# Layers 1 and 2 of the likelihood as 32x32 products in differing array tiles, with attention that subtracts its maxima

## The chip, the cores and the metric

The kernel runs on one NeuronCore of one Trainium2 chip. The metric is the device time of one execution in microseconds. A core has five engines that run side by side, each with its own queue in fixed order: TensorE (PE; PEld is its loading of weights), VectorE (DVE), ScalarE (ACT), GpSimd (POOL) and SyncE (SP), which issues most DMAs. PE writes to PSUM, a small memory of eight banks; DVE and ACT read it from there.

## What is computed

Two layers over x of shape 4 x 192 x 128 x 128 (batch, channels, 16384 pixels as tokens). The first is an attention block over tokens that are sorted by cluster; the second gives each value a likelihood.

```python
# layer 0, per image: tokens xn = layernorm(x^T), sorted by the nearest of 64 means
out1 = attn(q, k window of 256 keys, v window)      # groups of 128 queries, 8 heads of 24
out2 = attn(q, kg, vg)                              # 64 global keys per head
out = unsort(out1 + out2) @ Wproj @ Wconv
xt = x + out
h1 = layernorm(xt) @ W_fc1                          # 384 channels
xt = xt + gelu(depthwise_conv3x3(h1)) @ W_fc2
# layer 1, per channel: a chain of small maps, for lower = x - 0.5 and upper = x + 0.5
for i, (M, b) in enumerate(zip(Ms, bs)):            # 3x1, 3x3, 3x3, 1x3
    x = einsum('coi,cin->con', softplus(M), x) + b
    if i < 3:
        x = x + tanh(fs[i]) * tanh(x)
s = -sign(lower + upper)
result = maximum(abs(sigmoid(s * upper) - sigmoid(s * lower)), 1e-9)
```

`attn` is a softmax attention with scale 24 ** -0.5. In the likelihood a channel has three hidden values, so the maps of layers 1 and 2 are 3x3 per channel: 192 channels give 576 rows, and each map is block-diagonal.

## The kernel before

Everything is 32-bit. The program is written with a scheduling library that fixes the order of each engine's queue when it is built; buffers come from pools, and an instruction that takes a buffer waits for its last reader. PSUM has two rings: `ps1` gives one-bank tiles, four in number, and `ps2` gives two-bank tiles, two in number.

First weights are prepared. Then, for each of the four images, come these stages (functions by name):

- `cluster` normalises the tokens, finds each one's mean and its rank (lines 442 to 526); `order` scatters token numbers with 128 indirect DMAs on POOL (L533). Image 0's and 1's clustering comes at the start, that of images 2 and 3 before attention of images 1 and 2; `order` of the next image is issued beside `attention` of this one.
- `attention` (L628) walks 32 blocks of 512 sorted tokens. `fetch` gathers them (POOL, L553), `project` makes queries, keys and values (L562 to L564, L658 to L660), and for each tile of 128 keys `weigh` forms the scores `st` (eight products of 26 rows in different row tiles, L680) and `se` against the global keys (L689), and takes Exp on ACT (L683, L692). `gather` multiplies with the values (L705, L708), `divide` transposes (L719) and divides by the sums. Each step of the loop, `advance(g)`, does `weigh(g)`, `divide` of an older tile and `gather(g - 2)`. There are 4 x 128 tiles.
- `finish` (L758) walks 32 blocks of 512 pixels: `expand(i)`, `convolve(i - 1)`, `likelihood(i - 2)`. `expand` gathers the attention result, adds the residual, normalises and does fc1 (L787 to L800). `convolve` is nine multiply-adds per channel group on DVE (L821). `likelihood` does fc2 (L836) and the four maps.

The maxima. Softmax is taken without subtracting a maximum where a bound says that this is safe. The preparation computes such a bound from Gram matrices of the weights (`grams`, L182) and leaves a 0 or 1 in `wide`; the function `shifts` (L566), which computes maxima and writes them to `shifts_d` in memory, stands in a branch on it (L927). `project` loads the shifts from there into two spare rows per head of the queries (L645 to L649); they are zero when the branch isn't taken. In the profiled execution no instruction of `shifts` is in the trace.

The likelihood. Forty channels make a group of 120 rows; there are five groups, the last of 96 rows. Layer 0 is one product per group into a `ps1` tile (L859). Layers 1 and 2 are two products per group, one per side (lower, upper), with a 120x120 block-diagonal matrix (L866):

```python
ps = ps2(f"h{layer}_{n}_{g}")
for s in range(2):
    mm(ps[:m, s, :], lhsT=lw[:m, g].rearrange("p c o -> p (c o)")[:, :m],
       rhs=us[g][:m, s, :], start=True, stop=True)
us[g] = bend(g, layer, ps)
```

`bend` takes tanh of each side on ACT (L850) and then one multiply-add of both sides on DVE (L852), from PSUM; only then is the `ps2` tile free for the next group but one. Layer 3 (L874) sums three and two groups, and L878 to L888 make the likelihood with ACT, POOL and DVE.

A 32-bit product is two records in the trace, [...]so that L866 with 2 layers x 128 blocks x 10 products has 5120.

Of the kernel before, what the change touches and what calls it, by code (L numbers as in the profile page):

```python
# [31 lines left out]
R = 3 * G  # L32
NG = 5
HR = 32
LN_EPS = 1e-5
BOUND = 1e-9
SAFE = 60.0
# [3 lines left out]
def conv_seq_kernel(  # L41
# [73 lines left out]
    l0a = const([CA, 3, G, 3], "l0a")  # L115
    l0b = const([CB, 2, G, 3], "l0b")
    l1w = const([R, NG, G, 3], "l1w")
    l2w = const([R, NG, G, 3], "l2w")
    l3a = const([R, 3, CA], "l3a")
    l3b = const([R, 2, CB], "l3b")  # L120
    gate = const([R, 3, NG], "gate")
    bias = const([R, 3, NG, 2], "bias")
# [3 lines left out]
    def rows_of(g):  # L126
        return R if g < NG - 1 else 3 * (C - (NG - 1) * G)

    shifts_d = [dram.tile([8, 2, N], F32, tag=f"sh_d{b}", name=f"sh_d{b}") for b in range(B)]
    wide = const([1, 1], "wide", I32)

    with tc.tile_pool(name="prep", bufs=2) as prep:
# [42 lines left out]

        bounds = prep.tile([P, 2, 2], F32, bufs=1)  # L180

        def grams(parts, name):  # L182

            out = prep.tile([P, 2, HR], F32, tag=name, name=name, bufs=1)
            for t in range(2):
                ps = ps1("ps_gram")
                for k, part in enumerate(parts):
                    w = part[:, t].rearrange("p h e -> p (h e)")
                    mm(ps[:, 0:P], lhsT=w, rhs=w, start=k == 0, stop=k == len(parts) - 1)
                for h in range(4):  # L190
                    r = slice(HR * h, HR * h + HR)
                    nc.vector.tensor_copy(out[r, t], ps[r, r])
            return out

        gram_q = grams((q0, q1), "gram_q")
        gram_k = grams((k0, k1), "gram_k")
        nc.vector.tensor_tensor(gram_k, gram_k, gram_q, ALU.mult)
        nc.vector.tensor_reduce(bounds[:, 0], gram_k, AX.X, ALU.add)
# [54 lines left out]
        kgt = prep.tile([M, 2, 4, HR], F32, bufs=1)  # L253
        for t in range(2):
            ps = ps1("ps_kgt")
            mm(ps[:M, 0:P], lhsT=ma[:, 0, :], rhs=kp0[:, t].rearrange("p h e -> p (h e)"), start=True, stop=False)
            mm(ps[:M, 0:P], lhsT=mb[:, 0, :], rhs=kp1[:, t].rearrange("p h e -> p (h e)"), start=False, stop=True)
            nc.vector.tensor_copy(kgt[:, t].rearrange("p h e -> p (h e)"), ps[:M, 0:P])
        gram_m = grams((kgt,), "gram_m")
        nc.vector.tensor_tensor(gram_m, gram_m, gram_q, ALU.mult)  # L260
        nc.vector.tensor_reduce(bounds[:, 1], gram_m, AX.X, ALU.add)

        both = prep.tile([P, 2], F32, bufs=1)
        nc.vector.tensor_scalar_mul(both, bounds[:, 1], float(C + 1))
        nc.vector.scalar_tensor_tensor(both, bounds[:, 0], float(C + 1) ** 2, both, ALU.mult, ALU.add)
        ps = ps1("ps_bound")
        mm(ps[:, 0:2], lhsT=ones, rhs=both, start=True, stop=True)
        total = prep.tile([1, 1], F32, bufs=1)
        nc.vector.tensor_reduce(total, ps[0:1, 0:2], AX.X, ALU.add)
        nc.vector.tensor_scalar(total, total, SAFE * SAFE, None, ALU.is_le)  # L270
        nc.vector.tensor_scalar(total, total, -1.0, 1.0, ALU.mult, ALU.add)
        nc.vector.tensor_copy(wide, total)
        zeros = prep.tile([P, 16 * N // P], F32, bufs=1)
        nc.vector.memset(zeros, 0.0)
        for sh_d in shifts_d:
            nc.sync.dma_start(out=sh_d.rearrange("k t (a n) -> (k t a) n", n=16 * N // P), in_=zeros)
# [30 lines left out]

        NS = 8 * NG + 6
        raw = prep.tile([P, NS], F32, bufs=1)
        nc.vector.memset(raw, 0.0)  # L310
        rawg = raw[:, 0:8 * NG].rearrange("p (g e) -> p g e", e=8)
        vecs = prep.tile([R, 6, NG], F32, bufs=1)
        nc.vector.memset(vecs, 0.0)
        m0r = m0.rearrange("c (o u) -> (c o) u", u=1)
        for g in range(NG):
            n = rows_of(g)
            s = slice(g * R, g * R + n)
            nc.sync.dma_start(out=rawg[:n, g, 0:1], in_=m0r[s, :])
            nc.sync.dma_start(out=rawg[:n, g, 1:4], in_=m1[s, :])
            nc.sync.dma_start(out=rawg[:n, g, 4:7], in_=m2[s, :])  # L320
            nc.sync.dma_start(out=rawg[:n, g, 7:8], in_=m3[s, :])
            for e, v in enumerate((b0, b1, b2, f0, f1, f2)):
                nc.sync.dma_start(out=vecs[:n, e, g:g + 1], in_=v[s, :])
        nc.sync.dma_start(out=raw[:CA, 8 * NG:8 * NG + 3], in_=m0[0:CA, :])
        nc.sync.dma_start(out=raw[:CB, 8 * NG + 3:NS], in_=m0[CA:C, :])
        sp = prep.tile([P, NS], F32, bufs=1)
        e1 = prep.tile([P, NS], F32, bufs=1)
        u1 = prep.tile([P, NS], F32, bufs=1)
        c1 = prep.tile([P, NS], F32, bufs=1)
        nc.scalar.activation(e1, raw, AF.Abs)  # L330
# [297 lines left out]
    def attention(b, xn_d, idx, beside):  # L628

        at_d = dram.tile([N, C], F32, tag="at_d", bufs=2, name=f"at_d{b}")  # L630
        with tc.tile_pool(name=f"at{b}", bufs=2, reuse_waits="tile") as pool:
# [104 lines left out]
            def advance(g):  # L736
                if g < NT:
                    weigh(g)
# [237 lines left out]
```

## Time and profile before

| what | value |
|---|---|
| time, median of 3 runs | 14425.05 us (14421.28 to 14430.82) |
| profiled execution: time | 14425.05 us |
| profiled execution: span | 14423.3 us |
| mean granted PE clock | 0.885 of full |
| PE busy | 11673.1 us (81%) |
| DVE busy | 7433.7 us (52%) |
| ACT busy | 6510.6 us (45%) |
| POOL busy | 3611.5 us (25%) |
| L852, gates on DVE | 2416.4 us, 1920 of 1274 ns |
| L850, tanh on ACT | 2397.7 us, 3840 of 684 ns |
| L866, layers 1 and 2 on PE | 1204.4 and 1193.0 us, 2560 records each |
| L821, convolution on DVE | 2500.4 us, 5304 of 518 ns |

A share of the whole span is a mean over stages with different limits. So the stages have to be looked at one by one, and in each the question is which engine's queue has no gaps. Durations of one operation include its latency; two that follow each other on an engine start closer together than that. `idle before <- X` names what ended an engine's wait.

### The profile page before, as it was taken

The page shows a single profiled execution, that of the slowest core. Times are in us where ns is not written, and L with a number is a line of the kernel's source. Part 1 is how long each engine was busy: PE and PEld are TensorE (multiplying, and loading weights), DVE is VectorE, ACT ScalarE, POOL GpSimd, SP SyncE. Part 2 cuts the span into 40 slices and gives each one's busy share as a digit, 9 for nine tenths or more (in the row PEclk, how much of TensorE's full clock was granted, in tenths as well). Part 3 has the DMA queues.
Part 4 walks back from the last instruction along what each step waited for, and adds up shares of the span by engine and source line. Part 5 has one row for each costly group of instructions (what it writes and reads, how often), then busy time and mean ns, then how long its engine had stood idle before and what let it go on. Part 6 is the DMA issues. An engine that isn't in the chain of part 4 may idle for free. (4 is left out here: it accounts for less than half of the span.)

```text
span 14423.3 us, 161829 instructions
## 1 busy us (share of the span) xinstructions
PE 11673.1 (81%) x60928; PEld 5960.0 (41%) x60928; DVE 7433.7 (52%) x14065; ACT 6510.6 (45%) x9595; POOL 3611.5 (25%) x3991
## 2 busy tenths in 40 slices
PE   7658888888877888888887788888888888788888
PEld 5535543333354554333335455433333455333333
DVE  5611137777762113777775211477777111577776
ACT  1124445555522444555552244455555444455555
POOL 1443222222213322222212432222221222222222
PEclk6579999999967999999996799999999999899999
DMA  2200000000021000000002000000000000000000
GB/s 84 73 15 24 26 27 19 18 20 19 14 62 28 24 25 27 19 19 18 19 13 66 24 26 24 27 20 18 19 19 12 23 26 25 26 19 18 20 19 10
DMA packets 302035, 373.88 MB, mean 26 GB/s; under 512 B 58590, under 2 KB 208542, under 8 KB 300702
## 3 DMA queue, kind: packets, MB, share of 16 engines
q1 hardware_dynamic: 235678, 262.11, 6.1%
q0 software_dynamic: 65536, 101.02, 2.7%
q8 instruction: 491, 8.04, 0.2%
q14 instruction: 330, 2.70, 0.1%
HBM read 207.51 MB, written 155.45 MB: 25 GB/s over the span
## 5 line engine op out<-in xcount | busy, mean ns | idle before, releaser
L850 ACT ACTIVATE t_f<-h_f,bias 120x512 f32<-120x512 f32 (+1 forms) x3840 | 2397.7, 684 | 1711.6 <-PE h_f L866 1311.5
L821 DVE SCALAR_TENSOR_TENSOR acc_f<-hd_f,dwt,acc_f 128x128 f32<-128x128 f32 (+2 forms) x5304 | 2500.4, 518 | 568.1 <-ACT hd_f L800 521.3
L852 DVE SCALAR_TENSOR_TENSOR u_f<-t_f,gate,h_f 120x1024 f32<-120x1024 f32 (+1 forms) x1920 | 2416.4, 1274 | 244.0 <-ACT t_f L850 241.2
L866 PE MATMUL h_f<-u_f,l2w 120*120 120x512 f32 (+1 forms) x2560 | 1204.4, 606 | 247.5 <-DVE u_f L852 247.4
L683 ACT ACTIVATE es<-st 128x1024 f32<-128x1024 f32 (+1 forms) x1024 | 990.3, 1018 | 657.2 <-PE st L680 630.1
L722 DVE RECIPROCAL rec<-ao 128x16 f32<-128x16 f32 x512 | 131.9, 258 | 2143.4 <-PE ao L719 2102.5
L866 PE MATMUL h_f<-u_f,l1w 120*120 120x512 f32 (+1 forms) x2560 | 1193.0, 605 | 28.8 <-DVE u_f L852 28.8
L768 POOL DMA_INDIRECT at_f<-at_d,pos x512 | 615.1, 1201 | 2150.8 <-PE pb_gf L435 1900.7
L660 DVE COPY va_a<-pv_a 128x512 f32<-128x512 f32 x256 | 176.9, 692 | 1622.7 <-PE pv_a L659 1572.5
L728 POOL TENSOR_TENSOR ot<-on 128x192 f32<-128x192 f32 x512 | 303.5, 593 | 2544.4 <-DVE on L724 2541.1
L880 POOL TENSOR_TENSOR sg_f<-lu_f 120x512 f32<-120x512 f32 (+1 forms) x256 | 383.4, 1498 | 2186.5 <-ACT lu_f L878 2176.8
L798 PE MATMUL ph_f<-ta_f,fc 128*128 128x512 f32 x768 | 608.6, 886 | 395.7 <-ACT ta_f L433 395.7
L882 DVE TENSOR_TENSOR lu_f<-lu_f,sg_f 120x1024 f32<-120x1024 f32 (+1 forms) x256 | 317.4, 1240 | 1081.0 <-ACT sg_f L881 1081.0
L689 PE MATMUL se<-qt_a,kgx 64*128 64x128 f32 x4096 | 379.4, 305 | 596.0 <-ACT es L683 590.1
L866 PEld LDWEIGHTS h_f<-u_f,l2w 120*120 120x120 f32 (+1 forms) x2560 | 417.4, 178 | 1011.7 <-DVE u_f L852 627.0
L712 ACT COPY sums<-av 128x512 f32<-128x512 f32 x512 | 300.1, 586 | 1122.3 <-PE av L708 1031.1
L874 PE MATMUL h_f<-u_f,l3a 120*120 120x512 f32 x1536 | 692.2, 600 | 128.4 <-DVE u_f L852 128.4
L866 PEld LDWEIGHTS h_f<-u_f,l1w 120*120 120x120 f32 (+1 forms) x2560 | 441.3, 180 | 746.7 <-issue 602.6
L705 PE MATMUL av<-es,va_a 128*32 128x128 f32 x16384 | 712.9, 287 | 1.3 <-issue 1.3
L680 PE MATMUL st<-qt_a,kt_a 26*128 26x256 f32 (+1 forms) x8192 | 702.8, 406 | 3.0 <-issue 2.6
L836 PE MATMUL py_f<-acc_f,fc 128*120 128x512 f32 (+1 forms) x1536 | 680.7, 592 | 0.0
L533 POOL DMA_INDIRECT idx_d<-tok,pos x512 | 501.4, 979 | 700.9 <-DMA idx_d<-tok,pos 610.2
(307 smaller groups left out, 19364.0 us busy)
## 6 DMA issues: line engine op xcount, KB each, us to landing
xn_d<-xn_c SPq DMA_DIRECT2D x128, 384.0 KB
at_d<-ot SPq DMA_DIRECT2D x128, 384.0 KB
xa_c<-in_x SPq DMA_DIRECT2D x128, 256.0 KB
xa_f<-in_x SPq DMA_DIRECT2D x128, 240.0 KB
out<-pm_f SPq DMA_DIRECT2D x128, 240.0 KB
xb_f<-in_x SPq DMA_DIRECT2D x128, 144.0 KB
out<-pm_f SPq DMA_DIRECT2D x128, 144.0 KB
xb_c<-in_x SPq DMA_DIRECT2D x128, 128.0 KB
```

What stands on the lines that cost most here:

```text
L533: nc.gpsimd.indirect_dma_start(out=idx_d[:, :], out_offset=bass.IndirectOffsetOnAxis(ap=pos[:, t:t + 1], axis=0), in_=tok[:, t:t + 1], in_ ...
L680: mm(psv[:, h, t, :], lhsT=kt[r, t, ks], rhs=qt[r, t, c0 + q0_:c0 + 2 * P], start=True, stop=True)
L683: nc.scalar.activation(e[:, :, :, q0_:], psv, AF.Exp)
L705: mm(av[HR * r:HR * r + HR, 0, t, :], lhsT=blocks[k // NJ][2][:, k % NJ, 4 * t + r, :], rhs=es[r // 2][:, r % 2, t, c0:c0 + P], start=w == ...
L768: nc.gpsimd.indirect_dma_start(out=at[:, j, :], out_offset=None, in_=at_d[:, :], in_offset=bass.IndirectOffsetOnAxis(ap=pos[:, t:t + 1], a ...
L798: mm(ps, lhsT=fc1_0[:, s], rhs=ta, start=True, stop=False)
L821: nc.vector.scalar_tensor_tensor(acc[:, k, r0:r1, :], src[:, k, s0:s0 + r1 - r0, dx:dx + W], dwt[:, k, t:t + 1], acc[:, k, r0:r1, :], ALU. ...
L836: mm(ps[:m], lhsT=fc2[:, k, s], rhs=acc[:, k].rearrange("p r w -> p (r w)"), start=k == 0, stop=k == 2)
L850: nc.scalar.activation(t[:m, s, :], src[:m, s, :], AF.Tanh, bias=bias[:m, layer, g, s:s + 1])
L852: nc.vector.scalar_tensor_tensor(u[:m], t[:m], gate[:m, layer, g:g + 1], src[:m], ALU.mult, ALU.add)
L866: mm(ps[:m, s, :], lhsT=lw[:m, g].rearrange("p c o -> p (c o)")[:, :m], rhs=us[g][:m, s, :], start=True, stop=True)
L874: mm(ps[:m, s, :], lhsT=part[:r, k], rhs=us[g][:r, s, :], start=k == 0, stop=k == len(gs) - 1)
```

## The change

Two things differ from the kernel before.

In the likelihood, layers 1 and 2 become products of 32x32: a set of ten channels (30 of 32 rows) and one side each. A group of 40 channels lies as four sets in the four quarters of the 128 partitions, so a group and layer takes eight products. `turn` moves the output of layer 1 by a number of quarters that depends on group and side, so that the eight products of a group, and those of two groups in a row, fall into different 32x32 tiles of the array; layer 2 moves them back. Since the two sides then lie in different quarters, bias and gate get a side too, and the gate of layer 1 is two instructions of 512 elements. All tiles have 128 rows.

```diff
-                    t = pool.tile([R, 2, NB], F32, tag="t", bufs=2, name=f"t_{n}_{g}_{layer}")
+                    t = pool.tile([P, 2, NB], F32, tag="t", bufs=2, name=f"t_{n}_{g}_{layer}")
                     for s in range(2):
-                        nc.scalar.activation(t[:m, s, :], src[:m, s, :], AF.Tanh, bias=bias[:m, layer, g, s:s + 1])
-                    u = pool.tile([R, 2, NB], F32, tag="u", bufs=6, name=f"u_{n}_{g}_{layer}")
-                    nc.vector.scalar_tensor_tensor(u[:m], t[:m], gate[:m, layer, g:g + 1], src[:m], ALU.mult, ALU.add)
+                        nc.scalar.activation(t[:, s, :], src[:, s, :], AF.Tanh, bias=bias[:, layer, g, s:s + 1])
+                    u = pool.tile([P, 2, NB], F32, tag="u", bufs=6, name=f"u_{n}_{g}_{layer}")
+
+                    for v in ([slice(0, 1), slice(1, 2)] if layer == 1 else [slice(0, 2)]):
+                        nc.vector.scalar_tensor_tensor(u[:, v], t[:, v], gate[:, layer, g, v.start:v.start + 1],
+                                                       src[:, v], ALU.mult, ALU.add)
...
-                        for s in range(2):
-                            mm(ps[:m, s, :], lhsT=lw[:m, g].rearrange("p c o -> p (c o)")[:, :m],
-                               rhs=us[g][:m, s, :], start=True, stop=True)
+                        for q in range(Q):
+                            for s in range(2):
+                                r = 32 * ((q + turn(layer - 1, g, s)) % Q)
+                                c = 32 * ((q + turn(layer, g, s)) % Q)
+                                w = l1w[r:r + 32, g] if layer == 1 else l2w[r:r + 32, g, s]
+                                mm(ps[c:c + 32, s, :], lhsT=w, rhs=us[g][r:r + 32, s, :], start=True, stop=True)
                         us[g] = bend(g, layer, ps)
```

```python
def turn(layer, g, s):
    return 2 * (g % 2) + s if layer == 1 else 0
```

In attention the bound, the branch, `shifts` and `shifts_d` are gone; the maxima are computed in every case, inside the loop. `maxima(g)` forms the scores of 128 queries against 256 keys and against the global keys and reduces them on DVE; `shift(g)` transposes the maxima and subtracts them from the queries, once for each of the two key tiles that meet them (`pair`). `weigh` runs one tile later.

```diff
             def advance(g):
-                if g < NT:
-                    weigh(g)
+                mx = maxima(g) if g < NT else None
+                if 1 <= g <= NT:
+                    weigh(g - 1)
                 if late:
                     divide(*late.pop())
-                if 2 <= g < NT + 2:
-                    late.append((g - 2, gather(g - 2)))
+                if 3 <= g < NT + 3:
+                    late.append((g - 3, gather(g - 3)))
+                if mx is not None:
+                    shift(g, mx)
```

```python
def maxima(g):
    ...
    mx = pool.tile([P, 2, 4, HR], F32, tag="mx", name=f"mx{b}_{g}")
    nc.gpsimd.memset(mx, 0.0)
    for a in range(2):
        ps = ps2(f"sm{b}_{g}_{a}")
        psv = ps.rearrange("p h (t e) -> p h t e", t=2)
        for t in range(2):
            for h in range(2):
                r = slice(HR * (2 * a + h), HR * (2 * a + h) + D)
                mm(psv[:, h, t, 0:n], lhsT=qt[r, t, qs], rhs=kt[r, t, c0:c0 + n], start=True, stop=True)
        nc.vector.tensor_reduce(
            mx[:, :, 2 * a:2 * a + 2, D].rearrange("p t h -> p h t"), psv[:, :, :, 0:n], AX.X, ALU.max)
    ps = ps1(f"sg{b}_{g}")
    for t in range(2):
        mm(ps[:, t * 256:(t + 1) * 256], lhsT=qt[:, t, qs],
           rhs=kgx[:, t].rearrange("p h m -> p (h m)"), start=True, stop=True)
    nc.vector.tensor_reduce(mx[:, :, :, D + 1], ps.rearrange("p (t h m) -> p t h m", t=2, m=M),
                            AX.X, ALU.max)
    return mx

def shift(g, mx):
    ...
    for t in range(2):
        nc.tensor.transpose(pmv[:, t, :], mx[:, t].rearrange("p h e -> p (h e)"), ident)
    nc.vector.tensor_tensor(pair(g)[:, :, 1, :], qt[:, :, qs], pmv, ALU.subtract)
    if g + 1 < NT:
        nc.vector.tensor_tensor(pair(g + 1)[:, :, 0, :], qt[:, :, qs], pmv, ALU.subtract)
```

The buffers of the exponentials `es` go from eight to six, those of `eg` from four to three. In the preparation the small weights are loaded with fewer, longer DMAs, built per set of ten channels on partitions 0 to 31 and copied to their quarters.

## The prediction

> **What bounds the kernel now.** I read the page's slices first, then the groups, then each engine's timeline over one steady stretch of each stage.
>
> ```profile
> PE   7658888888877888888887788888888888788888
> DVE  5611137777762113777775211477777111577776
> PEclk6579999999967999999996799999999999899999
> ```
>
> Four pairs of stages are seen. Where DVE is at 1 it is attention (about 1130 us each: its L680 runs from 889 to 2014, 4464 to 5594, 8048 to 9175 and 11277 to 12342). Where DVE is at 7 it is the finish stage (about 2030 us each), which ends in the likelihood. Clustering fills the rest.
>
> ```profile
> 1400.00:1900.00 500.00, 434.35 (x4641) 274.67 (x4642) 68.30 (x148) 229.80 (x327) 104.74 (x148) 1.00 0.09 25
> 2200.00:3900.00 1700.00, 1396.96 (x3357) 550.98 (x3358) 1228.02 (x2055) 916.23 (x1359) 404.55 (x368) 0.91 0.07 18
> ```
>
> The columns are length, then PE, PEld, DVE, ACT and POOL busy, then clock. Attention is PE's alone: 87% against 14% on DVE. Finish has PE at 82% and DVE at 72%, and which of them is the bound is not read from such means. One query tile of attention, from the timeline of PE:
>
> ```profile
> 1505.71 1.16 PE L680 MATMUL st<-qt_a,kt_a 26*128 26x256 f32 x16
> 1507.97 0.72 PE L689 MATMUL se<-qt_a,kgx 64*128 64x128 f32 x8 [1.10 <-ACT es L683]
> 1508.62 0.66 PE L719 MATMUL ao<-ident,sums 128*128 128x128 f32 x4
> ...
> 1511.13 1.16 PE L680 MATMUL st<-qt_a,kt_a 26*128 26x256 f32 x16
> ```
>
> The loop takes 5.42 us per tile, with one wait of 1.1 us for Exp to free a two-bank PSUM buffer; projections add some 3.6 us per tile (1130 us / 128 tiles = 8.8). In finish a block of 512 pixels repeats every 63.5 us. Its DVE, while layers 1 and 2 run:
>
> ```profile
> 2957.18 1.66 DVE L821 SCALAR_TENSOR_TENSOR acc_f<-hd_f,dwt,acc_f 128x384 f32<-128x384 f32 x3
> 2959.13 1.28 DVE L852 SCALAR_TENSOR_TENSOR u_f<-t_f,gate,h_f 96x1024 f32<-96x1024 f32 x1 [0.29 <-ACT t_f L850]
> 2960.32 0.61 DVE L821 SCALAR_TENSOR_TENSOR acc_f<-hd_f,dwt,acc_f 128x384 f32<-128x384 f32 x1
> 2960.85 1.28 DVE L852 SCALAR_TENSOR_TENSOR u_f<-t_f,gate,h_f 120x1024 f32<-120x1024 f32 x1
> ...
> 2970.36 1.28 DVE L852 SCALAR_TENSOR_TENSOR u_f<-t_f,gate,h_f 96x1024 f32<-96x1024 f32 x1 [0.31 <-ACT t_f L850]
> 2978.86 1.23 DVE L882 TENSOR_TENSOR lu_f<-lu_f,sg_f 120x1024 f32<-120x1024 f32 x1 [7.22 <-ACT sg_f L881]
> ```
>
> From 2930.4 to 2971.6 DVE has only four gaps, 0.21, 0.44, 0.29 and 0.31 us: 1.25 us of 41. The convolution's L821 stands in its queue between the gates L852. PE, in the same stretch, waits for it:
>
> ```profile
> 2965.22 3.81 PE L866 MATMUL h_f<-u_f,l2w 120*120 120x512 f32 x8 [1.06 <-DVE u_f L852]
> 2970.10 5.41 PE L874 MATMUL h_f<-u_f,l3a 120*120 120x512 f32 x12 [1.07 <-DVE u_f L852]
> ```
>
> So DVE, not PE, sets the pace of layers 0 to 2. Only from L874 on (some 22 us of the block) does PE's time and the chain behind it count, and none of that is made shorter.
>
> **What the Trainium skill says.** "TensorEngine Tiling (Array Packing)", Key Properties: different array tiles load weights and multiply in parallel. The trace agrees: L680's records of 256 columns in four row tiles cost 702.8 us / 8192 = 86 ns each, against 406 ns for one from start to end and about 213 ns of streaming (half of L836's 430 ns pitch at 512 columns). The same page, PSUM Bottleneck: tiling speeds up TensorE but not the evacuation of PSUM. That is this finish stage. "TensorE: Matmul & The Clock Gate", Part 1: the clock falls to half after a window of 3413 ns that counts as idle. The trace agrees on the window and shows that half idle is enough:
>
> ```profile
> 2598.80:2602.21 3.41, 1.03 (x6) 1.00 0.00 0
> 2602.21:2605.62 3.41, 0.81 (x4) 0.50 0.16 32
> 2609.04:2612.45 3.41, 3.41 (x5) 0.50 0.00 0
> ```
>
> Here 30% busy (first figure after the length) was followed by half clock, which ended only after a full window. The window before these, 55% busy, kept the clock; one of 53% (1230.09 to 1233.51) lost it.
>
> **The change, part by part.**
>
> *Layers 1 and 2.* Removed: 20 products per block, 40 records, at 430 ns: (1204.4 + 1193.0) / 128 = 18.7 us of PE. Added: 80 products, 160 records, with eight different tiles per group. A tile runs two records of 427 ns, eight tiles side by side: about 0.9 us per group instead of 1.87, so 9 us per block; 4.7 if two groups fill all sixteen. PE gives up 9 to 14 us. On the path this is worth only what DVE waited, 1.25 us at most; walking the after order through DVE's queue (one L821 now stands between the last two gates) I find L874 starting 0.9 us earlier. The split of layer 1's gate into two halves costs nothing: starts of 512-element operations are 0.60 us apart (L789), of 1024-element ones 1.19. Rows 120 to 128 cost no time. Sum: -0.9 us x 128 = -115 us.
>
> *What a faster PE triggers.* A group arrives every 2.2 to 2.5 us and PE is busy about 1.0 of it (with its latency): 40 to 45%, below the half that kept the clock. I expect half clock by the end of layer 2. There it hides (1.8 us per group is what DVE's pace allows today), but L874 begins at half clock and has to wait for one aligned full window: 3.4 to 6.8 us at half speed, 1.7 to 3.4 us lost, all on the path to L878, L880, L882. With four chances in five: +2.0 us; some 0.3 us more where L787/L788 are caught. +2.3 x 128 = +295 us. If the clock holds, this is 0. Finish together: +180 us.
>
> *Attention with maxima.* Added per query tile on PE: eight products like L680 (0.96 us for sixteen records), two like L658 with 256 columns (4 x 0.21 = 0.85), two transposes (0.3, L719). On DVE: two reductions of 1024 (L523: 1.21 each), one of 512 (about 0.69, between L480 and L523), two subtractions of 256 (0.42, L482). DVE has room, but the two-bank PSUM buffers are two, and now take five users in a row instead of three: the score products wait for both reductions. Walked through: scores of the maxima 0 to 1.15; subtractions for the tile before end at 1.06; first reduction 1.25 to 2.5, second to 3.65; first `st` 2.6 to 3.45, its Exp to 4.77, second `st` 3.75 to 4.6; `se` 4.85 to 5.5; `ao` to 6.1, `av` to 8.0 (1.92 today), transposes to 8.3. With the reductions starting 0.2 us earlier it is 8.05. Instead of 5.42: +2.65 to +2.9, I take +2.75 x 512 = +1410 us. Bounds: +2.1 (PE work alone, the stall overlapped) and +3.6 (each wait once more): +1075 to +1850.
>
> *Gone or moved.* 1024 small loads of shifts on SP, the copy on POOL (its like for keys stays), the memset of `mx` on POOL (no such row; bounded by 0.3 to 0.6 us, ahead of the reductions by a tile). In three attentions POOL also issues `idx_d` at 2.4 us each, 128 times; they lost some 65 us each by it (1130 against 1064 in the fourth). A longer tile covers part: -60 us over three. The branch before each attention goes; clustering's tail (DVE alone for 27 us, PE idle) may overlap the next gather in two stages: -40, bounded by 0 and -60. Preparation: 50 loads become 20 at 0.43 us, the wait for the branch value goes: -15. Together -115.
>
> Sum: +1410 + 180 - 115 = +1475, on 14423.3 us of span and 1.75 us around it, which is the median of the runs as well: 15,900 us.
>
> **The rivals.**
> 1. The clock holds, or is regained in time: finish gains 115 to 190. 15,570 to 15,600. For it: four-row work in attention keeps 1.00. Against: a DVE-paced PE is below half busy.
> 2. Attention stalls once more per tile (the ring of two buffers, POOL's memset behind an `idx_d`): +3.6 us per tile and half clock there at times, 16,350. For it: POOL is at 50% in the first third; against: the memset is two tiles ahead.
> 3. The other side: PE's saving comes off finish in full, because groups no longer wait and DVE's gaps close. With sixteen tiles at once 14 us x 128 = 1790: 14,425 + 1410 - 115 - 1790 = 13,930. It decides from 10.2 us per block. For it: PE at 82% and DVE at 72%. Against: DVE's 41 us without gaps; L866 could vanish and that queue would still take 40.
> 4. Half of that: 4.5 us per block, as by a shorter tail: 15,150.
>
> **How the numbers follow.** 0.58 for the forecast, 0.22 for rival 1, 0.11 for 2, 0.04 for 3, 0.05 for 4. The forecast's own spread (2.4 to 3.1 us per tile, finish 0 to +400) is 15,600 to 16,200; with rival 1 and some of 2 the range is 15,500 to 16,250. A measurement of this kernel tells 0.2% (29 us) from nothing; only rival 3 is faster: 0.04, none ends within 0.2% (0.01), slower 0.95.
>
> **What would show it.** Right: attention near 1480 us each, DVE there near 45%, a wait of the score products for DVE's reductions; L866's successor at 9 us per block or less, DVE's stretch of 41 us nearly unchanged, a finish stage within 5% of 2030 us, PEclk lower there, and L874's records slower. Wrong: a finish below 1900 us (then PE was the bound), a clock of 0.91 or more there, or a tile loop outside 7.5 to 9 us.

## The result, and the profile after

The changed kernel takes 16190.95 us (median of 4 runs, 16156.76 to 16230.05), the kernel before 14423.17 us (14418.51 to 14430.82, 4 runs). The ratio is 1.1226, with a 95% interval of 1.1199 to 1.1253: slower by 12.3%, 1768 us. The profiled execution took 16156.76 us (span 16154.7), 1731 us more than that of before.

The slices of the page after (tenths in 40 equal slices, as before):

```profile
PE   6679997777777999777777799977777899977777
DVE  6534447777753444777775344477777344477776
PEclk6579998888867999888885799988888999988888
```

Attention now shows DVE at 3 to 5 instead of 1, and takes about 4 slices instead of 3. In the finish stages PEclk stands at 8 where it stood at 9. Measured from the first product of a stage to its last, the four attentions take 1571, 1573, 1574 and 1489 us (before: 1136, 1141, 1138, 1075), together 1717 us more. The four finish stages take 2066, 2045, 2042 and 2045 us (before: 2043, 2044, 2043, 2044), together 24 us more. The rest of the kernel takes some 10 us less. So nearly all of the loss is attention's, and nothing of it comes back in finish.

Two stretches of steady work, one of attention and one of finish (columns: length, PE, PEld, DVE, ACT and POOL busy, clock, DMA share, GB/s):

```profile
1500.00:2300.00 800.00, 778.40 (x6850) 486.96 (x6844) 334.35 (x515) 271.49 (x376) 142.16 (x239) 0.96 0.06 18
2700.00:4300.00 1600.00, 1206.55 (x6080) 408.39 (x6078) 1153.53 (x2032) 849.88 (x1265) 356.30 (x345) 0.82 0.07 19
```

Two things are to be read there. In finish PE is busy 75% (before 82%) at a clock of 0.82 (before 0.91), DVE 72% as before: PE was freed, and the stage did not get shorter. In attention the clock is 0.96 (before 1.00).

One query tile of attention after, from the timeline of PE (start, duration, then line and operation; in brackets the idle time before it and what ended it):

```profile
1726.47 1.16 PE L594 MATMUL sm<-kt_a,qt_a 24*128 24x256 f32 x16
1727.56 1.13 PE L599 MATMUL sg<-kgx,qt_a 128*128 128x256 f32 x4
1729.00 2.27 PE L631 MATMUL st<-qa,kt_a 26*128 26x256 f32 x16 [0.31 <-DVE mx L595]
1731.26 0.71 PE L640 MATMUL se<-qa,kgx 64*128 64x128 f32 x8
1731.90 0.65 PE L670 MATMUL ao<-ident,sums 128*128 128x128 f32 x4
...
1734.42 0.44 PE L612 MATMUL pm<-ident,mx 128*128 128x128 f32 x2
1734.79 1.16 PE L594 MATMUL sm<-kt_a,qt_a 24*128 24x256 f32 x16
```

The loop is 8.32 us (1734.79 - 1726.47) instead of 5.42. From start to start the difference is complete: `sm` 1.09, `sg` 1.13, a wait of 0.31 for the reductions, `pm` 0.37, together 2.90. The sixteen records of `st` took 1.16 us before, and then came 1.10 us of waiting for Exp; now they take 2.27 and the wait is gone. The same 2.26 us are spent in another way: DVE finishes its two reductions 1.1 us apart, so the first two row tiles run alone and then the other two, instead of all four side by side.

In finish, two groups of the page before (busy us, mean ns, then idle before and its releaser):

```profile
L866 PE MATMUL h_f<-u_f,l2w 120*120 120x512 f32 (+1 forms) x2560 | 1204.4, 606 | 247.5 <-DVE u_f L852 247.4
L874 PE MATMUL h_f<-u_f,l3a 120*120 120x512 f32 x1536 | 692.2, 600 | 128.4 <-DVE u_f L852 128.4
```

and the groups of the page after that answer to L866, L874 and L852:

```profile
L807 DVE SCALAR_TENSOR_TENSOR u_f<-t_f,gate,h_f 128x1024 f32<-128x1024 f32 (+1 forms) x2560 | 2484.6, 1007 | 129.9 <-ACT t_f L803 120.8
L824 PE MATMUL h_f<-u_f,l2w 32*32 32x512 f32 x10240 | 950.3, 809 | 473.0 <-DVE u_f L807 469.0
L824 PE MATMUL h_f<-u_f,l1w 32*32 32x512 f32 x10240 | 616.6, 706 | 130.0 <-DVE u_f L807 124.3
L830 PE MATMUL h_f<-u_f,l3a 128*120 128x512 f32 x1536 | 775.8, 660 | 203.8 <-DVE u_f L807 203.8
```

Layer 2's products fell from 1204.4 to 950.3 us of PE, layer 1's from 1193.0 to 616.6: 830 us, 6.5 us per block. PE's waits for the gates before layer 2 rose from 247.5 to 473.0 us. L830 (before L874) rose from 692.2 to 775.8 us by the lower clock, and the gates from 2416.4 to 2484.6 us by the two halves. What PE waits for is seen when DVE's timeline is laid beside it. PE waits 2.14 us before a group, while DVE goes from gate to convolution (L775, before L821) to gate without a gap:

```profile
3011.16 1.09 PE L824 MATMUL h_f<-u_f,l2w 32*32 32x512 f32 x16 [2.14 <-DVE u_f L807]
```

```profile
3008.30 1.40 DVE L775 SCALAR_TENSOR_TENSOR acc_f<-hd_f,dwt,acc_f 128x384 f32<-128x384 f32 x3
3009.62 1.40 DVE L807 SCALAR_TENSOR_TENSOR u_f<-t_f,gate,h_f 128x512 f32<-128x512 f32 x2
3010.93 0.61 DVE L775 SCALAR_TENSOR_TENSOR acc_f<-hd_f,dwt,acc_f 128x384 f32<-128x384 f32 x1
```

Over all full blocks (27 in each stage) DVE stands idle for 0.8 us of the 31.6 from a block's first layer 0 product to the start of layer 3; before, it was 1.1 of 31.8.

### The profile page after: what moved, and what is told of

It reads as the page before. It is cut to its first block, busy times and chain, and to the rows that moved or that the text cites. A ratio compares the mean times of both kernels' runs of the same rounds, so it can differ in the third digit from the quotient of the medians.

```text
span 16154.7 us, 217985 instructions
## 1 busy us (share of the span) xinstructions
PE 13107.1 (81%) x87582; PEld 6649.4 (41%) x87582; DVE 9394.2 (58%) x17398; ACT 6553.2 (41%) x9595; POOL 3667.6 (23%) x4495
## 5 line engine op out<-in xcount | busy, mean ns | idle before, releaser
L803 ACT ACTIVATE t_f<-h_f,bias 128x512 f32<-128x512 f32 x3840 | 2382.2, 685 | 1632.5 <-PE h_f L824 971.0
L775 DVE SCALAR_TENSOR_TENSOR acc_f<-hd_f,dwt,acc_f 128x128 f32<-128x128 f32 (+2 forms) x5304 | 2498.1, 517 | 528.4 <-ACT hd_f L754 478.1
L807 DVE SCALAR_TENSOR_TENSOR u_f<-t_f,gate,h_f 128x1024 f32<-128x1024 f32 (+1 forms) x2560 | 2484.6, 1007 | 129.9 <-ACT t_f L803 120.8
L631 PE MATMUL st<-qa,kt_a 26*128 26x256 f32 (+1 forms) x8192 | 1171.5, 417 | 306.1 <-DVE mx L595 306.0
L595 DVE TENSOR_REDUCE mx<-sm 128x4 f32<-128x1024 f32 (+1 forms) x1024 | 1202.3, 1217 | 288.4 <-PE sm L594 189.4
L824 PE MATMUL h_f<-u_f,l2w 32*32 32x512 f32 x10240 | 950.3, 809 | 473.0 <-DVE u_f L807 469.0
L631 PEld LDWEIGHTS st<-qa,kt_a 26*128 26x128 f32 x8192 | 714.2, 193 | 756.0 <-DVE mx L595 696.4
L830 PE MATMUL h_f<-u_f,l3a 128*120 128x512 f32 x1536 | 775.8, 660 | 203.8 <-DVE u_f L807 203.8
L613 DVE TENSOR_TENSOR qa<-qt_a,pm 128x256 f32<-128x256 f32 x512 | 215.5, 421 | 940.2 <-PE pm L612 878.5
L824 PE MATMUL h_f<-u_f,l1w 32*32 32x512 f32 x10240 | 616.6, 706 | 130.0 <-DVE u_f L807 124.3
L594 PE MATMUL sm<-kt_a,qt_a 24*128 24x256 f32 x8192 | 711.2, 405 | 8.6 <-issue 6.9
```

The source lines that it names most:

```text
L594: mm(psv[:, h, t, 0:n], lhsT=qt[r, t, qs], rhs=kt[r, t, c0:c0 + n], start=True, stop=True)
L595: nc.vector.tensor_reduce(mx[:, :, 2 * a:2 * a + 2, D].rearrange("p t h -> p h t"), psv[:, :, :, 0:n], AX.X, ALU.max)
L631: mm(psv[:, h, t, :], lhsT=kt[r, t, ks], rhs=qa[r, t, q0_:, :].rearrange("p w q -> p (w q)"), start=True, stop=True)
L775: nc.vector.scalar_tensor_tensor(acc[:, k, r0:r1, :], src[:, k, s0:s0 + r1 - r0, dx:dx + W], dwt[:, k, t:t + 1], acc[:, k, r0:r1, :], ALU. ...
L803: nc.scalar.activation(t[:, s, :], src[:, s, :], AF.Tanh, bias=bias[:, layer, g, s:s + 1])
L807: nc.vector.scalar_tensor_tensor(u[:, v], t[:, v], gate[:, layer, g, v.start:v.start + 1], src[:, v], ALU.mult, ALU.add)
```

## The experiments

All ratios are against the kernel before, run on the same chip, with their 95% intervals. For the two kernels of the change and four others, this is where the steps of a block of finish stand. They are means over 28 full blocks of the third finish stage (its first block and the last three are left out), worked out from the timeline of PE, in us after the block's first layer 0 product. `l3a` and `l3b` are the two parts of layer 3. The last column is the start of the next block.

```
kernel                        layer 1  layer 2   l3a    l3b   next block
before                          4.94    19.32   31.79  37.04    63.72
after                           5.12    18.62   31.36  37.41    63.58
before, gate of layer 1 split   4.97    19.35   31.90  37.15    63.73
before, two taps                4.63    18.43   30.55  35.80    62.15
tiles, two taps                 4.75    18.82   28.94  34.37    61.44
tiles, a product held ahead     6.40    24.96   37.89  43.14    67.96
```

**1. The tiles alone,** with all that belongs to them (the weights, 128 rows, the halved gate of layer 1).

```diff
# open: the kernel before, with the new likelihood
-                        for s in range(2):
-                            mm(ps[:m, s, :], lhsT=lw[:m, g].rearrange("p c o -> p (c o)")[:, :m],
-                               rhs=us[g][:m, s, :], start=True, stop=True)
+                        for q in range(Q):
+                            for s in range(2):
+                                r = 32 * ((q + turn(layer - 1, g, s)) % Q)
+                                c = 32 * ((q + turn(layer, g, s)) % Q)
+                                w = l1w[r:r + 32, g] if layer == 1 else l2w[r:r + 32, g, s]
+                                mm(ps[c:c + 32, s, :], lhsT=w, rhs=us[g][r:r + 32, s, :], start=True, stop=True)
```

> The kernel before with the likelihood in 32x32 tiles alone (attention still takes its shifts from the clustering pass). Theory: DVE's queue (convolution and gates) sets the pace of layers 0 to 2, so PE's 6 us per block come to nothing and the lower clock costs a little; the finish stages stay at 2040 to 2060 us each, time 14,400 to 14,480. Rival A (the tiles are worth their PE time, and the loss of the whole change hides it): 830 us of PE over 128 blocks, time 13,600 to 13,900. Rival B (the tiles cost 180 us by the half clock, as forecast): 14,550 to 14,650.

Measured: 14458.99 us, ratio 1.0025 (1.0016 to 1.0033), 37 us more. The theory's range holds, and the forecast's +180 us for finish doesn't. Its profiled execution took 14526.8 us, 68 above its median, so its stages aren't compared with the others; what made it longer is said in the next part.

**2. The maxima alone.** The diff is the reverse: the changed kernel with the old loop over `l1w` and `l2w`.

> The changed kernel with layers 1 and 2 as 120x120 block-diagonal products again. Theory: all of the loss is attention's, four stages of about 1570 us; PEclk in the finish stages back at 0.91; time 16,120 to 16,210. Rival (the tiles' lower clock in finish costs some hundred us): below 16,050. If the tiles save time in finish: above 16,300.

Measured: 16121.81 us, ratio 1.1174 (1.1155 to 1.1192), 1700 us more. This lies in the theory's range. Both halves add up to 1737 of 1768 us. The full blocks of finish are at 63.7 us again, as before. The loss is the maxima's.

**3. The gather between maxima and scores.**

```diff
                 mx = maxima(g) if g < NT else None
-                if 1 <= g <= NT:
-                    weigh(g - 1)
                 if late:
                     divide(*late.pop())
                 if 3 <= g < NT + 3:
                     late.append((g - 3, gather(g - 3)))
+                if 1 <= g <= NT:
+                    weigh(g - 1)
```

> The changed kernel; in each step of attention the division of one tile and the weighted sum of the next (L666 on) are issued between the maxima and the weighing, so that 2.6 us of PE work lies between the score products of the maxima and the st products that need their PSUM buffers. Theory (the st products wait for DVE's reductions through the ring of two, and the serialised halves lower the clock): the tile loop falls from 8.3 to 7.2 to 7.8 us, the clock in steady attention is back near 1.00, time 15,550 to 15,900. Rival A (PE's added work itself, with no wait that matters): unchanged, 16,100 to 16,200. Rival B (the wait only moves to se and to the next maxima, which want the same ring): 16,000 to 16,150.

Measured: 16013.4 us, ratio 1.1095 (1.1077 to 1.1114): 178 us better than the change, where the theory wanted 300 to 650. One tile of it, timeline of PE:

```profile
1711.92 1.16 PE L631 MATMUL st<-qa,kt_a 26*128 26x256 f32 x16
1714.18 0.72 PE L640 MATMUL se<-qa,kgx 64*128 64x128 f32 x8 [1.10 <-ACT es L634]
1714.82 0.44 PE L612 MATMUL pm<-ident,mx 128*128 128x128 f32 x2
1715.19 1.53 PE L594 MATMUL sm<-kt_a,qt_a 24*128 24x256 f32 x16
...
1720.08 1.16 PE L631 MATMUL st<-qa,kt_a 26*128 26x256 f32 x16
```

`st` runs in four row tiles again (1.16), but the 1.10 us for Exp are back at `se`, and `sm` is drawn out to 1.53: five users of a ring of two buffers hand the wait on. The loop is 8.16 us, and the clock from 1500 to 2300 us is 0.97, where the theory wanted nearly 1.00. Rival B described it; the theory's price was wrong.

**4. The kernel before, with its wait filled.**

```diff
                     es.append(e)
+                before_se()
                 ps = ps2(f"se{b}_{g}")
...
-                if g < NT:
-                    weigh(g)
-                if late:
-                    divide(*late.pop())
-                if 2 <= g < NT + 2:
-                    late.append((g - 2, gather(g - 2)))
+                def between():
+                    if late:
+                        divide(*late.pop())
+                    if 2 <= g < NT + 2:
+                        gather(g - 2, 0)
+                if g < NT:
+                    weigh(g, between)
+                else:
+                    between()
+                if 2 <= g < NT + 2:
+                    late.append((g - 2, gather(g - 2, 1)))
```

> The kernel before; in each step of attention the division (L719) and half of the weighted sum are issued between the second st and se, where PE waited 1.1 us for Exp to free a two-bank buffer. Theory (the ring of two is what attention waits for, with and without maxima): the loop falls from 5.42 to 4.4 to 4.6 us, 128 x 4 x 0.9 = about 450 us less, time 13,900 to 14,050. Rival (the wait moves to the next st, whose buffer is that of se): 14,300 to 14,430.

Measured: 13942.54 us, ratio 0.9665 (0.9649 to 0.9682), 479 us less. This lies in the theory's range, and this version is faster than both kernels. PE's timeline:

```profile
1615.79 1.16 PE L680 MATMUL st<-qt_a,kt_a 26*128 26x256 f32 x16
1616.88 0.66 PE L726 MATMUL ao<-ident,sums 128*128 128x128 f32 x4
1617.47 0.66 PE L709 MATMUL av<-es,va_a 128*32 128x128 f32 x16
1618.06 0.44 PE L712 MATMUL av<-eg,vgx 128*64 128x128 f32 x4
1618.43 0.71 PE L690 MATMUL se<-qt_a,kgx 64*128 64x128 f32 x8
```

No wait is left between `st` and `se`. From `ao` 1612.63 to `ao` 1616.88 the loop is 4.25 us, 1.17 below that of before; PE is busy for all of the stretch from 1400 to 1900 us. The loop alone would give 599 us; the four attentions became 486 us shorter, since the first three now last some 100 us longer than the fourth (before 63).

**5 and 6. A lighter DVE under both likelihoods.** The convolution has nine taps, of which the middle one is done on ACT and eight on DVE (L821). Six of these eight are left out in both kernels.

```diff
-                        if t == 4:
+                        if t < 3 or t == 4 or t > 5:
                             continue
```

> The kernel before with two of the convolution's eight taps on DVE; the other six are left out, so that L821 takes some 5 us of DVE per block instead of 19.5. To be read against the next run. Theory (DVE's queue paces layers 0 to 2): the finish stages fall until PE's own 52 us per block or the chain of Tanh and gate stops them; 13,300 to 14,000. Rival (a chain of PE, Tanh and gate paces them, whatever stands in DVE's queue): above 14,250.

> The 32x32 likelihood with attention as before, and the same six taps left out. Theory: with DVE's queue lighter, PE's 6 us per block count, and this kernel is 300 us or more below the kernel before with two taps. Rival (the products' time is hidden behind Tanh and gate, not behind the convolution): within 100 us of it, or above it.

Measured: 14232.69 us, ratio 0.9864 (0.9848 to 0.9880), and with tiles 14149.16 us, ratio 0.9807 (0.9791 to 0.9824). The theory fell in both: the first lies between it and its rival (above 14,250), the second where its rival wanted it (within 100 us). DVE's busy time fell by 1710 us (7433.7 to 5723.3), 13.4 us per block, and the block became only 1.6 us shorter; the tiles then bring 84 us, not 300. Layer 2's products, first with the old likelihood, then with tiles (timelines of PE):

```profile
3008.01 3.71 PE L866 MATMUL h_f<-u_f,l2w 120*120 120x512 f32 x8 [0.94 <-DVE u_f L852]
3012.66 3.70 PE L866 MATMUL h_f<-u_f,l2w 120*120 120x512 f32 x8 [0.94 <-DVE u_f L852]
```

```profile
3054.30 1.09 PE L902 MATMUL h_f<-u_f,l2w 32*32 32x512 f32 x16 [1.08 <-DVE u_f L885]
3055.99 1.09 PE L902 MATMUL h_f<-u_f,l2w 32*32 32x512 f32 x16 [0.60 <-DVE u_f L885]
3058.16 1.09 PE L902 MATMUL h_f<-u_f,l2w 32*32 32x512 f32 x16 [1.08 <-DVE u_f L885]
```

DVE now stands idle for 11.0 us up to l3a in the first kernel and for 9.0 in the second. Two groups take 4.65 us with the old products and 3.86 us with tiles, and PE still waits for a gate each time. This fits the turn of one buffer: product (1.87, or 1.09 with tiles), two Tanh (1.26), gate (1.28), then the next product may write it. That is 4.41 and 3.63 us, and with two buffers two groups per turn. No run has another number of buffers, so the ring as the cause is read from the timelines and not tested by itself. In the table, l3a starts at 28.94 instead of 30.55. So there is a second limit just below that of DVE's queue: with the old products 30.55 us without the convolution's queue and 31.79 with it; with tiles 28.94 against 31.36 (after). Of the 1.6 us that tiles gain in the layers, 0.9 are given back between l3a and the next block, where l3a and the products of L830 and L831 (fc1 of the next block; L798 and L799 in the kernel without tiles) run longer at half clock: over all full blocks L830 and L831 last 8.4 us instead of 7.9.

**7 and 8. Keeping the clock with products that nobody reads.**

```diff
+                        mm(ps1(f"wm{layer}_{n}_{g}"), lhsT=ident[:P, :], rhs=acc[:P, 0].rearrange("p r w -> p (r w)"),
+                           start=True, stop=True)
```

after each group of tiles; in the second kernel with 32 instead of `P` rows.

> The 32x32 likelihood with attention as before, and after each group of layers 1 and 2 one product of 128 rows and 512 columns whose result nobody reads (10 per block, 8.6 us of PE at full clock). Theory (the tiles lower the clock, and that costs what L830 shows, 0.65 us per block, and little else): PEclk in finish 0.90 or more, L830's records back to about 600 ns, time 14,340 to 14,420, at or under the kernel before. Rival A (the products added delay the true ones): above 14,500. Rival B (the clock costs nothing; the halved gate does): 14,440 to 14,480 with a high clock.

> The same as the run before, but the added products use 32 of the array's 128 rows; they take as long. Theory (the clock is kept by rows at work, not by a busy PE): PEclk in finish at 0.85 or less though the page shows PE as busy as with 128 rows, time 14,440 to 14,560. Rival (busy time keeps the clock): PEclk 0.90 or more, and the time of the run with 128 rows.

Measured: 15228.98 us, ratio 1.0556 (1.0538 to 1.0573), and 15324.48 us, ratio 1.0623 (1.0605 to 1.0640). The theories fell in both. The first lies in rival A's range (above 14,500), but not for rival A's reason: l3a starts at 30.7 us, earlier than in any kernel with the whole convolution. The reason was foreseen by none: the products take turns in the four one-bank buffers, and the planner then put the projection of the next block (`pr`) behind layer 3. Its normalisation waits in the tail (`pa` starts 53.4 us after the block's start instead of 45.2), and a full block takes 70.0 us in both. As a test of the clock they say little. The clock in the first finish stage is 0.89 with 128 rows and 0.88 with 32, so the second theory's 0.85 or less did not come, and the records of l3a are back at 600 ns and 608 ns.

**9. Another order for the maxima.**

```diff
                 for a in range(2):
+                    if a == 1:
+                        ps = ps1(f"sg{b}_{g}")
...
                     ps = ps2(f"sm{b}_{g}_{a}")
...
+                if late:
+                    divide(*late.pop())
+                if more:
+                    gather(g - 3, 0)
...
+                    weigh(g - 1, between)
```

where `between` issues the other half of the weighted sum ahead of `se`.

> The changed kernel; a step of attention is issued as sm, sg, sm, division, half of the weighted sum, st, st, the other half, se, transposes of the maxima, so that every wait for a two-bank PSUM buffer has other PE work before it. It tells how much of attention's loss is PE work and how much is waits. Theory (added PE work alone is 1.09 + 0.97 + 0.37 = 2.43 us per tile by the records of the run with the gather between; the rest, with the 1.1 us that the kernel before has too, is waits): tile loop 6.6 to 7.1 us, 15,250 to 15,500. Rival (the ring of two carries five users in any order; the wait moves again): loop 7.6 us or more, 15,750 or above.

Measured: 15916.86 us, ratio 1.1045 (1.1028 to 1.1062), 274 us better than the change but above the theory's 15,250 to 15,500. It is in the rival's range (15,750 or above), but without the rival's wait. One tile:

```profile
1710.55 1.13 PE L600 MATMUL sm<-kt_a,qt_a 24*128 24x256 f32 x8
1711.61 1.13 PE L591 MATMUL sg<-kgx,qt_a 128*128 128x256 f32 x4
1712.67 1.13 PE L600 MATMUL sm<-kt_a,qt_a 24*128 24x256 f32 x8
1713.74 0.66 PE L677 MATMUL ao<-ident,sums 128*128 128x128 f32 x4
...
1718.56 1.13 PE L600 MATMUL sm<-kt_a,qt_a 24*128 24x256 f32 x8
```

The loop is 8.01 us and no wait of note is left in it; the stretch from 1500 to 2300 us has a clock of 1.00. Neither side had this: with `sg` between its halves, `sm` costs 1.06 twice instead of 1.09 once, since eight records of two row tiles take as long as sixteen of four. Without that, the loop would be 8.01 - 1.03 = 6.98 us, an estimate that was not run. As run, the maxima cost 8.01 - 4.25 = 3.76 us per tile against experiment 4, and by the estimate still 2.7, some 1400 us. So with both kernels in the best order that was tried, the maxima's price is work of PE, not waits.

**10. Rows and the clock, alone.** Nothing of the reference is computed: products back to back on constant data, PE busy throughout, one execution. The rows of a product are the partitions that its input takes, of 128; `52*128` in a line means 52 rows and 128 columns.

```diff
+    for r in (96, 80, 64, 56, 52, 48, 44, 40, 32):
+        rows(P, 24, warm)
+        rows(r, 50)
+    for r in (64, 80, 88, 96, 112, 128):
+        rows(32, 24, warm)
+        rows(r, 50)
```

> No part of the reference is computed: stretches of 50 products back to back of 512 columns that use 96, 80, 64, 56, 52, 48, 44, 40 and 32 of the array's rows, each after 24 products of 128 rows; then 64 to 128 rows, each after 24 products of 32 rows; 128 rows by 32 columns; two and four row tiles of 26 rows in turn; groups of eight 32x32 products. PE is busy all the time. Theory (the clock counts rows): full clock holds down to a number of rows between 45 and 56, and falls to half below; from half it comes back only with some 90 rows or more; 128 rows by 32 columns keep it. Rival (the clock counts busy time): full clock in all stretches.

Timeline of PE, asked for in stretches of 20 us (x counts the records that begin in one; two records are one product):

```profile
299.60 20.76 PE L67 MATMUL bank<-rhs,ident 52*128 52x512 f32 x48
359.11 21.54 PE L67 MATMUL bank<-rhs,ident 48*128 48x512 f32 x25
1058.95 21.54 PE L67 MATMUL bank<-rhs,ident 88*128 88x512 f32 x25
1179.67 20.76 PE L67 MATMUL bank<-rhs,ident 96*128 96x512 f32 x48
1399.75 20.76 PE L79 MATMUL bank<-rhs,ident 128*32 128x512 f32 x48
1519.42 20.78 PE L86 MATMUL bank<-rhs,ident 26*128 26x512 f32 x192
```

48 records is full clock, 25 is half. From full clock, 52 rows keep it and 48 rows lose it; from half clock, 88 rows don't bring it back and 96 do. 128 rows by 32 columns keep it: columns don't count. Four row tiles in turn give 192 records, four at a time. The theory holds in these stretches, one for each number of rows, and a busy PE alone does not keep the clock. The groups of eight 32x32 products ran at 360 records in 18.90 us, 0.84 us per group.

**11. The split gate alone.**

```diff
-                    nc.vector.scalar_tensor_tensor(u[:m], t[:m], gate[:m, layer, g:g + 1], src[:m], ALU.mult, ALU.add)
+                    for v in ([slice(0, 1), slice(1, 2)] if layer == 1 else [slice(0, 2)]):
+                        nc.vector.scalar_tensor_tensor(u[:m, v], t[:m, v], gate[:m, layer, g:g + 1], src[:m, v],
+                                                       ALU.mult, ALU.add)
```

> The kernel before; only layer 1's gate (L852) is issued as two halves of 512 elements, as the tiles need it: 0.13 us more of DVE for each of 5 groups, 0.65 us per block. Theory (DVE's queue is on the path): 128 x 0.65 = 83 us more, 14,480 to 14,530. Rival A (costs nothing, as the prediction had it): within 20 us of the kernel before. Rival B (only the ring of two counts, where each half second gate is late by 0.13): 30 to 50 us more.

Measured: 14437.29 us, ratio 1.0015 (1.0009 to 1.0022), 22 us more. l3a is 0.11 us later, and the full block isn't longer (63.73 against 63.72). The 0.65 us of DVE per block do not reach the end of the block: up to l3a one L821 fewer stands in DVE's queue (22 instead of 23), so that DVE works 30.3 us there instead of 30.7. Each finish stage is some 4 us longer all the same, which must lie in its last blocks. Rival A comes closest, 2 us outside its range.

**12. A product held ahead of each group.**

```diff
                         ps = ps2(f"h{layer}_{n}_{g}")
+                        mm(ps[:, 0, :], lhsT=ident, rhs=fc2.rearrange("p k c -> p (k c)")[:, 0:NB], start=True, stop=True)
```

> The 32x32 likelihood with attention as before; each group of layers 1 and 2 begins with one product of 128 rows and 512 columns into its own PSUM buffer, which the true products then write over: 8.6 us of PE per block. No buffer is taken from others. Theory (the lower clock costs about 0.65 to 1 us per block after the layers, and DVE's queue hides the product): PEclk in finish 0.90 or more, L830's records (here L909) near 600 ns, 14,340 to 14,410. Rival (the ring of two two-bank buffers passes the product on to Tanh and gate): 14,450 to 14,560, though the clock is high.

Measured: 14977.98 us, ratio 1.0393 (1.0379 to 1.0408): above even the rival's range. Finish there, as in the second stretch above (its last 93 us lie behind the stage; from 2700 to 4000 us the clock is 0.92):

```profile
2700.00:4300.00 1600.00, 1310.03 (x6325) 469.16 (x6323) 1089.59 (x1947) 787.11 (x1172) 334.42 (x322) 0.90 0.07 21
```

The clock is back and every l3a takes 5.41 us. But layers 1 and 2 take 37.89 - 6.40 = 31.49 us instead of 26.24 after. An estimate for most of it: of ten products of 0.86 us, half come onto the path through a ring of two (4.3 us). Layer 1 also begins 1.3 us later, with the first two held products issued early; that part was not separated. DVE's queue does not hide it.

## Why the prediction was right, and where it was off

The direction was right, and its reason: attention pays for the maxima, and finish pays nothing back. 15,900 us was 291 us too low. That 16,190.95 lies inside 15,500 to 16,250 is in part luck: had finish cost the 180 us that were put down for it, the time would have been above the range. By its steps:

- *Attention, tile loop, +2.75 us.* Measured +2.90. Its parts were off in opposite ways: the added work was put at 0.96 + 0.85 + 0.3 = 2.11 and is 1.09 + 1.13 + 0.37 = 2.59; for the wait that left 0.64, and it is 0.31. The ring of two was seen rightly as the place of the wait, and that it would run `st` in two halves, too.
- *Attention outside the loop.* This is the step that failed by most: 1410 us were forecast, for the loop alone, and 1717 came. The loop accounts for 2.90 x 512 = 1485. What was put at nothing is a lower clock, which rival 2 alone allowed for. Over the four whole stages it is 0.930, 0.929, 0.933 and 0.960 (before 0.962, 0.961, 0.963 and 0.994). The time lost by it, (1 - clock) x length, comes to 387 us after and 137 before, if PE were busy throughout: 250 us more, an estimate, for the 232 that the loop leaves. "Four-row work in attention keeps 1.00" was rival 1's argument; it overlooked that the two halves of `st`, one after the other, put two row tiles to work at a time, not four. Three windows of 3.41 us, one after the other, show it (PE busy, then clock):

```profile
1633.30:1636.71 3.41, 3.10 (x25) 1.00 0.00 0
1636.71:1640.12 3.41, 3.41 (x36) 0.50 0.02 5
1640.12:1643.53 3.41, 3.41 (x42) 1.00 0.00 0
```

  In the first, PE is busy for 3.10 of 3.41 us, with `st` in halves (from 1634.12), and the second is at half clock. What tells such windows apart is the work of rows. As an estimate, each record counts with its columns (429 ns for 512, the pitch of experiment 10) times its rows of 128, summed over a window. In the stretch from 1500 to 2300 us the 17 windows that were followed by half clock come to 36 to 42% (the first one shown to 41%), and 198 of the 200 that kept it to 40% or more. Experiment 9, with `st` in four row tiles and no wait, has none below 44% there, and a clock of 1.00.
- *Gone or moved, -115 us.* Nearly nothing came (the rest outside both stages is about -10 us). That a longer tile would cover POOL's issues of `idx_d` was wrong: the first three attentions are 84 us longer than the fourth (1573 against 1489), before 63.
- *Layers 1 and 2, -115 us.* Right where the clock held. The 108 full blocks after, sorted by the start of l3a (means in us; the clock from the trace's record):

```
l3a starts at     blocks   half clock in first 12 us   DVE idle until l3a   next block
30.9                 43               0.0                     0.3             62.4
31.1 to 31.6         34               0.0                     0.5             64.3
32.7 to 33.1         31               1.9                     2.1             65.6
before: 31.8        108               0.0                     1.1             63.7
```

  In the first group l3a starts 0.9 us earlier than before, as forecast: the tiles take up DVE's waits, and no more can be had from a queue without gaps. In the mean of all blocks 0.2 us are left. "So DVE, not PE, sets the pace" is not all of it, though. Experiments 5 and 6 show a second limit 1.2 us below DVE's queue, at 30.55, which the tiles lower to 28.94. One sign of being right did not come: L866's successor takes (950.3 + 616.6) / 128 = 12.2 us of PE per block, not 9 or less.
- *The gate's halves at nothing.* Right within what can be measured: 22 us for the kernel, none for the block (experiment 11).
- *The half clock, +295 us.* The clock fell as forecast, to 0.82. Where it costs was seen in part only. l3a begins at half clock in 49 of 128 blocks, not in four of five, and then takes 7.11 us instead of 5.41. That is 0.38 x 1.70 = 0.65 us per block, where 2.0 were put down, because the window at half clock often ends while layer 2 still waits (in one block, groups of layer 2 take 1.96 and 1.9 us each from 3012.79 on, and l3a at 3020.65 takes 5.41). But half clock also delays the layers, which the forecast held to be hidden: in the third group, whose blocks all have 1.8 to 2.1 us of it in their first 12 us, l3a starts 2.0 us later than in the first. (Of the second group, 29 of 34 blocks have l3a itself at half clock, of the first none.) In all, the mean block takes 63.9 us and that of the first group 62.4. So about 1.5 us per block, 195 us, is an estimate of the half clock's price; it sorts blocks by their outcome. This uses up what the first group gains (1.35 us per block, 173 us), and +24 us are left in finish. The longer execution that was profiled in experiment 1 has 47 of 108 blocks in the third group and a mean block of 64.3 us.
- *Rival 3* (PE's saving comes off in full, 13,930) is excluded by experiment 1, and by experiment 6 even for a light DVE.

The errors in finish and attention had opposite signs (156 us too much, 307 too little). Two slips in the working changed nothing of note: the lower end of rival 1 is 14,425 + 1410 - 115 - 190 = 15,530, not 15,570, and projections add 8.8 - 5.42 = 3.4 us per tile, not 3.6.

Experiment 12 holds the clock and loses 4.4 us per block against the change (67.96 against 63.58). Half clock at about 1.5 us per block is cheaper than the products that were put on the ring's path.

## What to carry to other kernels

When PE waits, ask whose buffer it waits for before giving it less to do: the turn of a ring of two (product, Tanh, gate) and a full queue on another engine can stand 1 us apart, and a faster product then moves little. Where several users share such a ring, put independent products between them, which in the kernel before was worth 3.3%; but keep products of different row tiles adjacent, since they only overlap with their neighbours in the queue. A product added to keep the clock takes a buffer or a turn, and in all three trials cost more than the clock. A faster product also leaves PE idle for longer, and the half clock that follows can take back what it gained, as in finish here.

## What the runs showed of the hardware

A busy PE does not by itself keep the clock; the number of rows at work counts. The Trainium skill, "TensorE: Matmul & The Clock Gate", Part 1, has the full clock come "After ≥1 busy SHORT window" and the half clock "after ≥1 idle window". The runs differ in what is busy: with PE busy without a break, 48 of 128 rows (38%) lose the full clock and 52 (41%) keep it; 88 rows (69%) don't regain it in 86 us, and 96 (75%) do. Two row tiles of 26 rows in turn, 52 rows together, keep it as well (96 records in 20 us, two at a time). Columns don't count: 32 of 128 columns at 128 rows keep it. This fits the windows of attention in which a PE busy for 91% was followed by half clock. It also answers the prediction's "half idle is enough". By the same estimate as for attention, the window before the change that was 55% busy and kept the clock comes to 39%, and the one that was 53% busy and lost it to 16%.
